# Registers loaded once per stretch, and another layout of buffers and last writes, in a two-layer graph network kernel on one Trainium2 core

## The chip, the cores and the metric

The kernel runs on one core of one Trainium2 chip. The metric is the device time of one execution in microseconds (us), taken over several executions. Engines are named as in the profile: PE (matrix products), PEld (its weight loads), DVE (VectorE), ACT (ScalarE), POOL (GpSimd), SP (SyncE, which here only issues DMAs). "ACTq", "DVEq" and "POOLq" are the instruction queues of these engines: work that a queue does itself, such as loading registers from SBUF.

## The reference

There are 6250 nodes with 128 features, and 200,000 edges with 128 features each, sorted by their destination node. `dst` is 6250 times the square of a uniform number, so low nodes have many edges. Cut to what matters:

```python
def layer0(h, edge, src, dst, W, b):
    agg_src  = segment_sum(h[src], dst, 6250)
    agg_edge = segment_sum(edge, dst, 6250)
    return relu(concat([h, agg_src, agg_edge], 1) @ W.T + b)

def sage(h, src, dst, W_l, b, W_r):
    agg = segment_sum(h[src], dst, 6250) / maximum(degree(dst), 1)
    return agg @ W_l + b + h @ W_r

h = relu(layernorm(x));  x = x + layer0(h, edge_attr, src, dst, W, b)
h = relu(layernorm(x));  h = relu(sage(h, ..., W1_l, b1, W1_r))
x = x + relu(sage(h, ..., W2_l, b2, W2_r))
```

All three layers sum over the same edges. A matrix of counts (how many edges go from node s to node d) can therefore be built once and multiplied with each layer's features.

## The kernel before

**Two stages.** The *build* (0 to about 717 us) makes the count matrix and writes it to DRAM (`counts_d`), sums the edge features per destination (`aggE`), and computes the first layer's node products. The *layers* (from about 726 us) read the count matrix back, one block of 128 destinations at a time, 49 blocks for each of three layers, and multiply it with the features.

**Groups, units, stretches.** The edges are cut into 196 groups of 1024, each of 8 tiles of 128 edges. A *unit* is n tiles that share one window of destinations: n is 4 for groups 0 to 27, 2 for groups 28 to 83 and 1 for groups 84 to 195. For each group DVE makes one-hots (`onehots`, L440; `weigh`, L450): `sp` of the source's place in its block and `sq` of destination and block. PE multiplies them (L597; L609 adds what the tile before carries over when n is 1) into the PSUM tile `pu`, which holds two units; there are three such tiles. A count of three source blocks is packed into one 32-bit word, so a destination has 17 words (NJ).

ACT copies each unit's window from `pu` into a *ring*, an SBUF tile of up to 210 destinations (L624 for n = 1; L629, with L619 and an addition on POOL at L627, for n of 2 or 4). Where it goes in the ring depends on the data, so the place is a register, loaded from `at_i` by `group_values` (L433), once for each group: 8 neighbouring registers for n = 1, every second or fourth element of `at_i` for n of 2 or 4. For n above 1 POOL loads the same places for its additions. A *stretch* is as many groups as fill one ring: 14, 7, 4, 3 or 2; in the last six regions of 14 groups, 3, 3, 3, 3 and 2. At its end POOL writes the ring to `counts_d` (L647), from the stretch's first node, which it loads with `value` (L428). The rings rotate over three buffers. Ring writes overlap in DRAM, so each waits until the one before has landed. There are 70 of them. For the very last one the ring is cleared first (L559).

**Edge sums.** Beside the counts, `edge_sums` loads 512 KB of edge features per group on SP's queue (L482, five buffers), multiplies them by a one-hot on PE (L493, tile `pe`), and DVE adds the result into `aggE` at a place from a register (L498), loaded with `value` for each group (L428). `sum_edges` sets the order of these products among the count products on PE. One block of the first layer's node products follows every third group, until group 145.

**Between the stages.** The build's pools are closed and the layers' pools opened in the same SBUF: `terms` (features as a high and a low part, split by ACT at L704 and by DVE or POOL at L706, with two columns of ones set at L662), `loads` (three blocks of counts, read by `load_counts`, L505, on SP), `wides` (blocks widened to fp32 by DVE and ACT, L697). A tile of the new pools waits for what used its bytes before. Block 0's counts go into `c_early`, a tile of its own, read on POOL's queue after stretch EARLY - 1. The last six stretches are left out of that wait; a test on the data (`bad`) makes sure that they begin behind block 0, and otherwise all is computed again by `general`, another function, which does not run on these inputs. `neighbours` then multiplies, 49 products for each block (L753), and `windows_right`, whose first loads and memsets (L835 to L856) stand early in POOL's queue, tests the windows.

The order of instructions on each engine is set by the scheduler of the framework, by dependences and program order.

Of the kernel before, what the change touches and what calls it, by code (L numbers as in the profile page):

```python
# [23 lines left out]
P = 128  # L24
D = 128
U = 8
# [10 lines left out]
NONE = 2047.0  # L37
RUN = 14
XB = 4


REGIONS = (
# [20 lines left out]
def kernel(ctx: ExitStack, tc: tile.TileContext, x, srcl, dstl, edge, w0t, b0, w1l, b1, w1r, w2l, b2, w2r, out):  # L63
# [32 lines left out]
    for g0, g1, *reg in regions:  # L96
        for g in range(g0, g1, reg[2]):
            stretches.append((g, min(reg[2], g1 - g), *reg))
    NS = len(stretches)
    EARLY = NS - 6  # L100

# [86 lines left out]
    si = 0  # L188
    for g0, g1, n, w, k, sw, win in regions:
        nc.gpsimd.memset(room[:, g0:g1], float(sw - w))  # L190
        m = -(-(g1 - g0) // k)
        nc.gpsimd.memset(most[:, si : si + m], float(sw - 1))
        si += m
    make_identity(nc, ident)
# [146 lines left out]
    for end, u in ((0, 0), (GU + 1, GU - 1)):  # L341
# [3 lines left out]
    nc.vector.memset(worse, 0.0)  # L345

    nc.vector.tensor_scalar(
        bad[:, 1:2], starts[:, NS - 1 : NS], -1.0, float(NC * P - stretches[-1][5]), op0=ALU.mult, op1=ALU.add
    )
    nc.vector.tensor_scalar(  # L350
        bad[:, 3:4], starts[:, EARLY : EARLY + 1], -1.0, float(P), op0=ALU.mult, op1=ALU.add
    )
    setup.close()

# [58 lines left out]
    ring_of = [rings.tile([P, SWMAX * NJ], I32, name=f"ring{i}") for i in (2, 1)]  # L413
# [5 lines left out]
    ring_of.append(rings.tile([P, SWMAX * NJ], I32, name="ring0"))  # L419
    padded.append(rings.tile([P, HP], F32, name="hot2"))  # L420
    ring_of.reverse()
    padded.reverse()
    for t in ring_of[:1] + padded + ring_of[1:]:
        nc.gpsimd.memset(t.bitcast(F32), 0.0)
    bpsum = build.enter_context(tc.tile_pool(name="bpsum", bufs=2, space=bass.MemoryType.PSUM))

    def value(ap, engine, most):
        return nc.values_load(  # L428
            ap, engines=[engine], min_val=0, max_val=most, skip_runtime_bounds_check_because="clamped on the chip"
        )  # L430

    def group_values(ap, engine, most):
        _, values = nc.values_load_multi_w_load_instructions(  # L433
            ap, engines=[engine], min_val=0, max_val=most, skip_runtime_bounds_check_because="clamped on the chip"
        )
        return values
# [17 lines left out]
    def carries():  # L454
# [19 lines left out]
            carry[:, 0:1], flat_q[:, T1 - 2 : T1 - 1], pu[:, 0:1].unsqueeze(2).to_broadcast([P, 1, 2]), op=ALU.subtract  # L474
        )

    def edge_sums(g):
# [12 lines left out]
        ps = bpsum.tile([P, 512], F32, name="pe", bufs=2)  # L490
        for u in range(U):
            behind = yield
            mm = nc.tensor.matmul(ps[:, :P], e[:, u, :], hot[:, u * win : u * win + P], start=u == 0, stop=u == U - 1)  # L493
# [10 lines left out]
    def load_counts(queue, c, b):  # L504
        return queue.dma_start(c, counts_d[:, b * P * NJ : (b + 1) * P * NJ].rearrange("p (d k) -> p d k", k=NJ))  # L505
# [49 lines left out]
    for si, (g0, ng, n, w, k, sw, win) in enumerate(stretches):  # L555
        nq = NJ * w
        ring = ring_of[si % 3]
        if si == NS - 1:
            nc.gpsimd.memset(ring[:, : sw * NJ].bitcast(F32), 0.0)  # L559
        if before is not None and n > 1:  # L560
# [2 lines left out]
        for g in range(g0, g0 + ng):  # L563
# [8 lines left out]
                weigh(sq[:, :, :even], g, even)  # L572
            else:
                weigh(sp, g, P)
            places = at_i[0:1, g * U : (g + 1) * U : n]
            to_put = group_values(places, ET.Activation, (sw - w) * NJ)
            if n > 1:
                to_add = group_values(places, ET.Pool, (sw - w) * NJ)
            else:

                of_first = 2 if g == G1 else 1
                sc = hots.tile([P, U + 1, NJ + NJ % 2], BF16, name="sc")
                c0 = g * U - T1 + 1
                onehots(
                    sc[:, 2 - of_first : U + 1], carry[:, c0 + 1 - of_first : c0 + U], U + of_first - 1, NJ + NJ % 2
                )
            live = [t for t in range(0, U, n) if g < G - 1 or (t + n) * P > unused]
            many = 2 if nq <= 512 else 1
            for j in range(0, len(live), many):
                units = live[j : j + many]  # L590
                pu = bpsum.tile([P, 2 * 512], F32, name="pu", bufs=3)
                for i, t0 in enumerate(units):
                    for t in range(t0, t0 + n):
                        c = i * 512
                        while c < i * 512 + nq:
                            z = min(c // 512 * 512 + 512, i * 512 + nq)
                            mm = nc.tensor.matmul(  # L597
                                pu[:, c:z],
                                sp[:, t, :],
                                sq[:, t, c - i * 512 : z - i * 512],  # L600
                                start=t == t0,
                                stop=t == t0 + n - 1 and (n > 1 or c > i * 512),
                            )
                            c = z
                    if n == 1:

                        slot = t0 + 1 if t0 != live[0] else 1
                        for j0, (sp_b, t) in enumerate(last_tiles):
                            mm = nc.tensor.matmul(  # L609
                                pu[:, i * 512 : i * 512 + NJ],  # L610
                                sp_b[:, t, :],
                                sc[:, slot + 1 - len(last_tiles) + j0, :NJ],
                                start=False,
                                stop=j0 == len(last_tiles) - 1,
                            )
                    last_tiles = [(sp, t) for t in range(t0, t0 + n)]
                if n > 1:
                    fore = hots.tile([P, 2, NJ], I32, name="fore", bufs=8)
                    nc.scalar.copy(  # L619
                        fore[:, : len(units), :], pu.rearrange("p (i c) -> p i c", c=512)[:, : len(units), :NJ]  # L620
                    )
                for i, t0 in enumerate(units):
                    if n == 1:
                        nc.scalar.copy(ring[:, bass.ds(to_put[t0], nq)], pu[:, i * 512 : i * 512 + nq])  # L624
                        continue
                    to = ring[:, bass.ds(to_add[t0 // n], NJ)]
                    add = nc.gpsimd.tensor_tensor(to, to, fore[:, i, :], op=ALU.add)  # L627
                    tc.add_to_no_dep_group(f"add{si}", add.ins)
                    put = nc.scalar.copy(  # L629
                        ring[:, bass.ds(to_put[t0 // n] + NJ, nq - NJ)], pu[:, i * 512 + NJ : i * 512 + nq]  # L630
                    )
# [12 lines left out]
            begin = 0  # L644
        else:
            begin = value(first_i[0:1, g0 : g0 + 1], ET.Pool, N - 1) * NJ
        write = nc.gpsimd.dma_start(counts_d[:, bass.ds(begin, sw * NJ)], ring[:, : sw * NJ])  # L647
# [552 lines left out]
```

## Time and profile before

| what | value |
|---|---|
| time, median of 3 runs | 1696.02 us (1693.77 to 1696.36) |
| profiled execution | 1698.32 us; its span 1696.7 us |
| granted TensorE clock, mean | 0.977 |
| PE busy | 1561.9 us (92%) |
| DVE busy | 1303.3 us (77%) |
| ACT busy | 869.3 us (51%) |
| POOL busy | 297.3 us (18%) |
| groups 0 to 27 (n = 4), by the span | 48 to 115 us |
| groups 28 to 83 (n = 2) | 115 to 303 us |
| groups 84 to 195 (n = 1) | 303 to 717 us |
| last edge product to first product of block 1 | 715.7 to 744.0 us |

The profile is of one execution. Busy time counts what an engine computes; register loads, branches, semaphores and DMA issues are not counted, though they take an engine's queue. The "chain" is the work that ended last, followed back from the last instruction, at each step to what released it. In a list of waits the three numbers are us in total, times, and the longest. In the order of time an instruction's line has its start, its length, and in brackets how long its engine idled before it and who ended that.

### The profile page before, as it was taken

Reading aid. Unit: us, or ns where it says so; the run is one execution under the profiler, and the core shown is the slowest. Engines: PE = TensorE matmul, PEld = TensorE weight load, DVE = VectorE, ACT = ScalarE, POOL = GpSimd, SP = SyncE. Lnnn points to the kernel's source line nnn. Section 1 sums busy time; section 2 is a strip of 40 time slices with the busy share of each in tenths; the row PEclk is TensorE's granted clock in tenths of the full one; section 3 lists DMA queues with packets and bytes.
Section 4 is the critical chain, followed back from the end, with each engine's and each line's share of the span. In section 5 each row is a group of like instructions: output and inputs, shape, how many; then the busy total and the mean of one; then the engine's idle time right before and its main releaser. Section 6 shows DMA issues by size and latency. Waiting matters only on the chain.

```text
span 1696.7 us, 38957 instructions
## 1 busy us (share of the span) xinstructions
PE 1561.9 (92%) x13563; PEld 1506.6 (89%) x13563; DVE 1303.3 (77%) x2810; ACT 869.3 (51%) x2183; POOL 297.3 (18%) x657
## 2 busy tenths in 40 slices
PE   5998887889988888779999999899999999999998
PEld 5897777778878877669999999899999999999998
DVE  9887776678878778777777777888676777777775
ACT  3434443566766666655555555554444453444442
POOL 2534555200000000131211222201000020000000
PEclk9999998999999999979999999999999999999999
DMA  1877766678877788766666567455555556666662
GB/s 61 261 255 252 246 224 220 237 259 278 284 274 273 276 294 311 270 230 209 199 204 214 199 222 227 169 185 199 196 189 202 185 174 206 228 219 220 221 223 97
DMA packets 122572, 377.02 MB, mean 222 GB/s; under 512 B 15249, under 2 KB 67151, under 8 KB 99712
## 3 DMA queue, kind: packets, MB, share of 16 engines
q1 hardware_dynamic: 98676, 289.00, 51.2%
q0 software_dynamic: 15088, 80.80, 12.9%
q10 hardware_dynamic: 8604, 4.66, 0.9%
q8 instruction: 109, 1.79, 0.4%
q14 instruction: 95, 0.78, 0.2%
HBM read 289.94 MB, written 84.45 MB: 221 GB/s over the span
## 4 chain that ended last, share of the span: by engine, by line
PE 69%; ACT 11%; issue 7%; ACTq 4%; DVE 4%; DMA 3%; POOL 1%; POOLq 1%; DVEq 0%
PE ps L753 50%; PE pe L493 10%; ACT ring L624 9%; ACTq L433 4%; PE pu L597 3%; DMA counts_d<-ring 3%; PE pz L394 2%; PE pu L394 1%; PE pt L296 1%; PE pt L387 1%; PE ps L751 1%; ACT ring L629 0%; DVE sq L440 0%; DVE sp L440 0%; DVE w_n L247 0%
## 5 line engine op out<-in xcount | busy, mean ns | idle before, releaser
L753 PE MATMUL ps<-terms,wide 128*128 128x256 f32 (+1 forms) x7203 | 939.7, 290 | 20.0 <-DVE terms L706 13.0
L753 PEld LDWEIGHTS ps<-terms,wide 128*128 128x128 f32 x7203 | 905.5, 198 | 26.4 <-issue 13.2
L697 DVE CAST wide<-c 128x1024 fp32r<-128x1024 uint8 (+1 forms) x584 | 524.2, 907 | 145.8 <-PE ps L753 145.3
L697 ACT CAST wide<-c 128x1024 fp32r<-128x1024 uint8 x292 | 361.5, 1238 | 294.3 <-PE ps L753 233.5
L493 PE MATMUL pe<-hot,edge_t 128*128 128x128 f32 x3136 | 490.2, 293 | 8.8 <-DVE aggE L498 5.0
L493 PEld LDWEIGHTS pe<-hot,edge_t 128*128 128x128 f32 x3136 | 406.2, 196 | 15.2 <-DVE aggE L498 6.2
L624 ACT CAST ring<-pu 128x170 f32 (+6 forms) x891 | 256.1, 289 | 135.3 <-PE pu L609 57.4
L597 PE MATMUL pu<-sq,sp 128*128 128x136 bf16 (+8 forms) x1563 | 200.3, 225 | 61.5 <-ACT ring L624 37.3
L597 PEld LDWEIGHTS <-sp 128*128 128x128 bf16 x1563 | 135.6, 100 | 32.4 <-issue 25.8
L440 DVE TENSOR_TENSOR sp<-iota,p_e 128x1024 bf16<-128x1024 f16 x196 | 134.9, 688 | 37.5 <-PE pu L597 20.6
L440 DVE TENSOR_TENSOR sq<-iota,q_e 128x1088 bf16<-128x1088 f16 (+8 forms) x196 | 141.8, 723 | 13.2 <-PE pu L609 12.1
L398 POOL DMA_DIRECT2D r_d<-r x98 | 53.4, 545 | 506.4 <-DVE r L397 484.3
L609 PEld LDWEIGHTS <-sp 128*128 128x128 bf16 x892 | 80.7, 97 | 57.9 <-issue 51.6
L627 POOL TENSOR_TENSOR ring<-ring,fore 128x17 int32 x280 | 101.8, 363 | 116.0 <-ACT fore L619 37.8
L609 PE MATMUL pu<-sc,sp 128*128 128x17 bf16 x892 | 112.5, 173 | 0.0
L629 ACT CAST ring<-pu 128x119 f32 (+5 forms) x280 | 65.8, 245 | 75.8 <-issue 34.1
L647 POOL DMA_DIRECT2D counts_d<-ring x70 | 37.9, 542 | 374.5 <-ACT ring L624 310.4
L450 DVE TENSOR_TENSOR sp<-sp,w_e 128x1024 bf16<-128x1024 bf16 x140 | 95.9, 685 | 0.0
L484 DVE TENSOR_TENSOR hot<-iota,rel 128x64 f32<-128x64 f16 (+13 forms) x196 | 94.2, 484 | 0.0
L498 DVE TENSOR_TENSOR aggE<-aggE,pe 128x8 f32 (+13 forms) x196 | 37.7, 193 | 56.7 <-PE pe L493 38.2
L397 DVE TENSOR_TENSOR r<-pz,b_sb 128x128 f32<-128x128 f32 x98 | 28.0, 286 | 67.1 <-ACT feats L395 66.7
L772 DVE TENSOR_REDUCE y<-ps 128x128 f32<-128x256 f32 x147 | 60.9, 415 | 8.4 <-PE ps L753 8.4
(167 smaller groups left out, 961.1 us busy)
## 6 DMA issues: line engine op xcount, KB each, us to landing
c<-counts_d SPq DMA_DIRECT2D x146, 1088.0 KB, 5.0
edge_t<-in_edge SPq DMA_DIRECT2D x196, 512.0 KB, 4.6
own<-r_d SPq DMA_DIRECT2D x147, 64.0 KB, 1.8
counts_d<-ring POOLq DMA_DIRECT2D x5, 1785.0 KB, 7.9
counts_d<-ring POOLq DMA_DIRECT2D x5, 1598.0 KB, 8.2
counts_d<-ring POOLq DMA_DIRECT2D x5, 1462.0 KB, 8.0
counts_d<-ring POOLq DMA_DIRECT2D x5, 1377.0 KB, 6.2
r_d<-r POOLq DMA_DIRECT2D x98, 64.0 KB, 2.1
```

The costliest lines, as they stand in the source:

```text
L433: _, values = nc.values_load_multi_w_load_instructions(ap, engines=[engine], min_val=0, max_val=most, skip_runtime_bounds_check_because="c ...
L440: nc.vector.tensor_tensor(to.rearrange("p t (c two) -> p t c two", two=2), iota[:, :m].rearrange("p (c two) -> p c two", two=2).unsqueeze( ...
L450: nc.vector.tensor_tensor(pairs, pairs, w_e[:, g].bitcast(BF16).unsqueeze(2).to_broadcast([P, U, m // 2, 2]), op=ALU.mult)
L484: nc.vector.tensor_tensor(hot[:, : U * win].rearrange("p (u w) -> p u w", w=win), iota[:, :win].unsqueeze(1).to_broadcast([P, U, win]), re ...
L493: mm = nc.tensor.matmul(ps[:, :P], e[:, u, :], hot[:, u * win : u * win + P], start=u == 0, stop=u == U - 1)
L597: mm = nc.tensor.matmul(pu[:, c:z], sp[:, t, :], sq[:, t, c - i * 512 : z - i * 512], start=t == t0, stop=t == t0 + n - 1 and (n > 1 or c ...
L609: mm = nc.tensor.matmul(pu[:, i * 512 : i * 512 + NJ], sp_b[:, t, :], sc[:, slot + 1 - len(last_tiles) + j0, :NJ], start=False, stop=j0 == ...
L624: nc.scalar.copy(ring[:, bass.ds(to_put[t0], nq)], pu[:, i * 512 : i * 512 + nq])
L627: add = nc.gpsimd.tensor_tensor(to, to, fore[:, i, :], op=ALU.add)
L629: put = nc.scalar.copy(ring[:, bass.ds(to_put[t0 // n] + NJ, nq - NJ)], pu[:, i * 512 + NJ : i * 512 + nq])
L697: copy(t[:, : p1 - p0], two)
L753: dense = nc.tensor.matmul(ps[:, :m], wide[i, q][:, p, :, two], terms[:, s, :m], start=s == 0, stop=s == NB - 1)
```

## The change

The diff has six parts.

1. The places of a whole stretch are loaded into registers by one instruction at its first group (on ACT, and on POOL for n above 1), not by one for each group. An instruction loads up to 28 registers.
2. `edge_sums` loads the first nodes of 14 groups by one instruction on DVE.
3. The last stretch (groups 194 and 195) is cut in two, of one group each, so there are 71. The very last write takes 64 destinations and not 210.
4. The pools are opened in another order: edge tiles and the one-hots' tiles first, rings last, so that `terms` and `loads` lie where no ring was.
5. The one-hots' pool (`hots`, for `sp`, `sq` and `sc`) has three buffers in place of two.
6. The count loads of blocks 1 to 3 no longer wait for the last six ring writes; the test on the data now asks that these begin behind the first four blocks of the order (nodes 0 to 639).

```diff
+TAIL = 64
+AHEAD = 4
+FIRSTS = 14
...
+    g, ng, *reg = stretches.pop()
+    stretches += [(g, ng - 1, *reg), (g + ng - 1, 1, *reg)]
     NS = len(stretches)
     EARLY = NS - 6
...
     nc.vector.tensor_scalar(
-        bad[:, 1:2], starts[:, NS - 1 : NS], -1.0, float(NC * P - stretches[-1][5]), op0=ALU.mult, op1=ALU.add
+        bad[:, 1:2], starts[:, NS - 1 : NS], -1.0, float(NC * P - TAIL), op0=ALU.mult, op1=ALU.add
     )
     nc.vector.tensor_scalar(
-        bad[:, 3:4], starts[:, EARLY : EARLY + 1], -1.0, float(P), op0=ALU.mult, op1=ALU.add
+        bad[:, 3:4], starts[:, EARLY : EARLY + 1], -1.0, float((max(order[:AHEAD]) + 1) * P), op0=ALU.mult, op1=ALU.add
     )
...
+    edges = build.enter_context(tc.tile_pool(name="edges", bufs=5))
+    zeroed = build.enter_context(tc.tile_pool(name="zeroed", bufs=1))
+    hots = build.enter_context(tc.tile_pool(name="hots", bufs=3))
     rings = build.enter_context(tc.tile_pool(name="rings", bufs=1))
-    hots = build.enter_context(tc.tile_pool(name="hots", bufs=2))
-    edges = build.enter_context(tc.tile_pool(name="edges", bufs=5))
...
-    padded = [rings.tile([P, HP], F32, name=f"hot{i}") for i in range(2)]
...
+    padded = [zeroed.tile([P, HP], F32, name=f"hot{i}") for i in range(3)]
+    ring_of = {(NS - i) % 3: rings.tile([P, SWMAX * NJ], I32, name=f"ring{i}") for i in (3, 2, 1)}
...
-        base = value(first_i[0:1, g : g + 1], ET.DVE, N - 1)
-        to = aggE[:, bass.ds(base, win)]
+        if g % FIRSTS == 0:
+            bases[:] = group_values(first_i[0:1, g : min(g + FIRSTS, G)], ET.DVE, N - 1)
+        to = aggE[:, bass.ds(bases[g % FIRSTS], win)]
...
+        wide_write = sw if si < NS - 1 else TAIL
...
-            places = at_i[0:1, g * U : (g + 1) * U : n]
-            to_put = group_values(places, ET.Activation, (sw - w) * NJ)
-            if n > 1:
-                to_add = group_values(places, ET.Pool, (sw - w) * NJ)
-            else:
+            if g == g0:
+                places = at_i[0:1, g0 * U : (g0 + ng) * U : n]
+                to_put = group_values(places, ET.Activation, (sw - w) * NJ)
+                if n > 1:
+                    to_add = group_values(places, ET.Pool, (sw - w) * NJ)
+            if n == 1:
...
-                        nc.scalar.copy(ring[:, bass.ds(to_put[t0], nq)], pu[:, i * 512 : i * 512 + nq])
+                        nc.scalar.copy(ring[:, bass.ds(to_put[(g - g0) * U + t0], nq)], pu[:, i * 512 : i * 512 + nq])
...
-        write = nc.gpsimd.dma_start(counts_d[:, bass.ds(begin, sw * NJ)], ring[:, : sw * NJ])
+        write = nc.gpsimd.dma_start(counts_d[:, bass.ds(begin, wide_write * NJ)], ring[:, : wide_write * NJ])
         if si >= EARLY:
             tc.declare_no_dep(write.ins, group="early", reason="it begins behind the first block, or all is computed again")
+            tc.add_to_no_dep_group("behind", write.ins)
...
-        load_counts(nc.sync, c, blocks[i][1])
+        load = load_counts(nc.sync, c, blocks[i][1])
+        if i < AHEAD:
+            tc.declare_no_dep(load.ins, group="behind", reason="they begin behind these blocks, or all is computed again")
```

More of the change, by code (lines that the diff above doesn't have):

```diff
@@ L190 @@
         nc.gpsimd.memset(room[:, g0:g1], float(sw - w))
-        m = -(-(g1 - g0) // k)
+        m = sum(g0 <= s[0] < g1 for s in stretches)
         nc.gpsimd.memset(most[:, si : si + m], float(sw - 1))
@@ L406, in load_x @@
         return xt
+    edges = build.enter_context(tc.tile_pool(name="edges", bufs=5))
+    zeroed = build.enter_context(tc.tile_pool(name="zeroed", bufs=1))
+    hots = build.enter_context(tc.tile_pool(name="hots", bufs=3))
     rings = build.enter_context(tc.tile_pool(name="rings", bufs=1))
-    hots = build.enter_context(tc.tile_pool(name="hots", bufs=2))
-    edges = build.enter_context(tc.tile_pool(name="edges", bufs=5))
-    ring_of = [rings.tile([P, SWMAX * NJ], I32, name=f"ring{i}") for i in (2, 1)]
     HP = U * WINMAX + P - WINMAX
     HP += HP % 2
-    padded = [rings.tile([P, HP], F32, name=f"hot{i}") for i in range(2)]
[L419 to L423, printed above, removed]
+    padded = [zeroed.tile([P, HP], F32, name=f"hot{i}") for i in range(3)]
+    ring_of = {(NS - i) % 3: rings.tile([P, SWMAX * NJ], I32, name=f"ring{i}") for i in (3, 2, 1)}
+    for t in [ring_of[0], *padded, ring_of[1], ring_of[2]]:
         nc.gpsimd.memset(t.bitcast(F32), 0.0)
@@ L475, in carries @@
         )
+    bases = []
     def edge_sums(g):
@@ L623 @@
                     if n == 1:
-                        nc.scalar.copy(ring[:, bass.ds(to_put[t0], nq)], pu[:, i * 512 : i * 512 + nq])
+                        nc.scalar.copy(ring[:, bass.ds(to_put[(g - g0) * U + t0], nq)], pu[:, i * 512 : i * 512 + nq])
                         continue
-                    to = ring[:, bass.ds(to_add[t0 // n], NJ)]
+                    to = ring[:, bass.ds(to_add[((g - g0) * U + t0) // n], NJ)]
                     add = nc.gpsimd.tensor_tensor(to, to, fore[:, i, :], op=ALU.add)
@@ L629 @@
                     put = nc.scalar.copy(
-                        ring[:, bass.ds(to_put[t0 // n] + NJ, nq - NJ)], pu[:, i * 512 + NJ : i * 512 + nq]
+                        ring[:, bass.ds(to_put[((g - g0) * U + t0) // n] + NJ, nq - NJ)], pu[:, i * 512 + NJ : i * 512 + nq]
                     )
```

## The prediction

> **What bounds the kernel now.** The page's chain first, then the same chain for the part that the change touches most, 303 to 717 us, where one tile makes one unit (n = 1). Its line shares:
>
> ```profile
> PE ps L753 50%; PE pe L493 10%; ACT ring L624 9%; ACTq L433 4%; PE pu L597 3%; DMA counts_d<-ring 3%; PE pz L394 2%; PE pu L394 1%; PE pt L296 1%; PE pt L387 1%; PE ps L751 1%; ACT ring L629 0%; DVE sq L440 0%; DVE sp L440 0%; DVE w_n L247 0%
> ```
> ```profile
> by line: ACT ring L624 37.3%; PE pe L493 18.9%; ACTq L433 11.7%; issue 11.6%; PE pu L597 6.6%; DMA counts_d<-ring 4.0%; PE pu L394 1.5%; ACT h L376 1.2%; PE pu L609 1.0%; ACTq L624 0.8%; DVE sq L440 0.8%; DMA x_c<-in_x 0.8%; DVE sp L440 0.6
> ```
>
> Half the span is the layers (L753, PE alone, from 744 us on); no instruction there changes. In the n = 1 part ACT's ring copies lead, and ACTq L433, the loading of registers in ACT's queue, holds 11.7% of 414 us = 48 us of the chain. PE's waits from 302 to 717 say who pays:
>
> ```profile
> PE pu L597 <- ACT ring L624: 37.3, 64, 2.4
> ```
>
> Why a load of eight registers is sometimes long: one stretch of three groups, ACT's and POOL's order of time, then busy times by group (length; PE, PEld, DVE, ACT, POOL; clock; DMA share; GB/s).
>
> ```profile
> L433 ACTq TENSOR_LOAD <-at_i x4: 546/548/2152, 594.8 to 605.7; - x4
> ```
> ```profile
> 595.56 2.63 ACT L624 CAST ring<-pu 128x170 f32 x8 [0.45 <-PE pe L493]
> 600.25 2.63 ACT L624 CAST ring<-pu 128x170 f32 x8 [2.06 <-issue]
> 603.32 2.63 ACT L624 CAST ring<-pu 128x170 f32 x8 [0.45 <-PE pe L493]
> ```
> ```profile
> 595.40 0.53 POOL L647 DMA_DIRECT2D counts_d<-ring  x1 [10.45 <-ACT ring L624]
> ```
> ```profile
> 594.80:597.90 3.10, 3.10 (x38) 2.85 (x34) 2.95 (x7) 2.42 (x9) 0.53 (x1) 1.00 0.63 153
> 597.90:602.60 4.70, 3.23 (x38) 2.85 (x33) 3.04 (x7) 2.42 (x9) 0.00 (x0) 1.00 0.98 397
> 602.60:605.65 3.05, 3.05 (x36) 2.80 (x33) 2.90 (x7) 2.38 (x9) 0.00 (x0) 1.00 0.81 290
> ```
>
> The load that opens a stretch takes 0.55 us: the last ring write has landed and the next is not yet moving. The second group's load, 2.5 us after POOL issued the write, takes 2.15 us: the DMA queue of the ring writes holds 65% of the engines just then. ACT pauses 2.06 us, PE idles 1.47. With a short load a group takes 3.05 to 3.10 and PE never idles. By the trace's load records the three places of a stretch average 0.55, 1.81 and 0.69 us (last six regions); all 112 loads sum to 114 us where 0.547 each would be 61.
>
> **The change, part by part.** (1) *ACT's registers, n = 1.* 112 loads become 45: 24 of 24 registers, 19 of 16, 2 of 8, each at a stretch's head, in the quiet place. Price of 24 neighbouring registers: one takes 0.30 (L428 on DVE), eight 0.547, so 35 ns for each further one: 1.11 us; 16: 0.83. Bounds: 0.55 (length is free) and three eights, 1.64. The quiet place lasts about 2.1 us (last copy 0.3, POOL's issue 0.53, 1.2 until bytes move), so I take 1.11. The stretch then needs on ACT 24 copies 0.332 apart in the chain's order of time = 7.97, a restart of 0.42 and 0.56 more load = 8.95 us; on PE 3.10 + 3.23 + 3.05 = 9.38; on DVE 8.89. It took 10.85: PE would set 9.4.
>
> All PE idle in this part is (152.4 - 133.8) + (261.8 - 226.7) = 54 us (windows 302.8 to 455.2 and 455.2 to 717): the upper end. Lower end: ACT still decides, and of the chain's 48 us the new loads keep 24 x 0.81 + 19 x 0.53 + 2 x 0.25 = 30 (length less the 0.30 behind the last copy): gain 18. PE decides in my stretch, but ACT and DVE are within 5% of it, and from 455 us DMA is busy 0.81 of 261.8 = 212 us, a floor. I take 36, two thirds of 54.
>
> A rule speaks against this. Row: 4 registers apart from each other (n = 2) take 0.89, 2 take 0.474, so 0.21 to 0.24 each, but 8 neighbours 0.547, 0.07 each. The Trainium skill, "Runtime: NRT & Kernel Launch", section "Instruction fetch mechanics", has a register load cost about 200 ns per register "even for bulk". By it a 24-register load would be 4.8 us and the 896 registers 179 us instead of the 114 traced: some 65 us slower. The row of eight is a third of the rule, so the sum goes by the row.
>
> (2) *DVE's first_i, 14 at a time.* 182 of 196 loads go. Short ones (0.30) hide behind the one-hots ahead; the long ones (1.29 at 608.7) fall in the same writes as ACT's. Nothing added to (1): they are inside PE's idle sum. A 14-register load is 0.76 (0.30 to 2.4 by strided rows), 14 times: nothing. *The third one-hot buffer* removes waits of DVE for PE: of `sp` and `sq` (L440) 26 us from 300 to 717. PE itself waited for DVE only 6.7 us there (aggE 5.0, r 1.4, hot 0.3), which bounds the gain; a loss would need more work, and there is none. It mostly keeps DVE's 8.89 off a 9.4 path: 2 won (0 to 7).
>
> (3) *n = 4 and n = 2 (48 to 303 us).* As many registers as before, apart from each other, so no cheaper: 28 cost about 6 us, 16 about 3.5, 8 about 1.8, in lumps. The first lump, 6 us from 45 on POOL and 47 on ACT, lies beside 6.15 us of edge products on PE (48.6 to 54.8), which wait for neither: nothing, and 3 us lost if that cover is short. In n = 2 ACT's lump of 3.5 us holds up PE only beyond the three pu tiles, 1.5 groups, 4.3 us. POOL's lump stands behind its write's issue, where loads of four already take 1.6 to 2.5 us; queued behind it are the ring additions and the next write. Loads hold 6.8% + 3.3% of 187 us = 19 us of this part's chain. Bounds: half of that won, 10; or 23 stretches each half a us later, 12 lost. Taken: 2 won.
>
> (4) *The handover.* Before, everything waited for the last ring write:
>
> ```profile
> 711.26 8.09 DMA counts_d<-ring
> 719.98 5.96 DMA counts_d<-ring
> 732.19 4.69 DMA limits_d<-limit
> 740.07 3.92 PE ps L753 x18
> ```
>
> PE ends the build at 715.7; the write lands at 725.9; block 0 stalls on POOL's two splits (behind rows, limit) at half clock; block 1 begins at 743.9. In the built order of the change, splits and ones column no longer wait for rings, but every *widened* piece of block 0, on DVE and ACT, still waits for the last write, and there is one write more. The write of 194 is still 210 wide and cannot go before 719.4, when its predecessor lands; ahead of it on POOL stand the ones column and four row loads (2.7 us from 715.9), which fit. Three loads of 1088 KB run beside it from 717: 3.34 + 1.83 MB at the 0.42 MB/us of the windows 728 to 734 end at 729.3, or at 726 if the write goes first. Then the short write: 557 KB = 1.33 us plus the 1.6 that 5.96 leaves over 1.83 MB: about 3. It lands between 729 and 734; I take 732. The first piece is there 0.85 later, block 0 takes 8.0 (20 products at the half clock's 0.218, 3.92 over 18; 29 at 0.122, as later blocks have them), block 1 begins near 741: 2.5 won, between 2 lost and 6 won. The early loads themselves win little: block 1's were there in time before too.
>
> Sum: 36 + 2 + 2 + 2.5 = 42.5. Profiled execution 1698.3 less 42.5 = 1655.8; it lies 2.3 over the median shown: 1653.5, given as 1654.
>
> **Rivals.** (a) *DMA and DVE take over.* A group's DMA work, 2.8 to 3.2 us from 455 us on, meets a period of 3.1; writes then lag, edge tiles come late. Against it: PE idles least in groups with short loads, though DMA is 0.63 to 0.81 busy there. Gain 8 to 28, near 1678. 0.20. (b) *Slower: a register costs the same alone or in bulk.* If each beyond the eighth costs the strided 0.22, a 24-register load is 4.1 us, 1 us more than a stretch's three loads now (3.05), and in one lump longer than PE's lead of three pu tiles (six of eight units, 2.3 us); 43 stretches x about 1 us, and n = 2 no better: near 1735. It decides from 0.16 us per further register. For it the strided rows; against it the row of eight. 0.08. (c) *More than PE's share returns*: with no long pauses the half-clock spells go too (clock 0.90 from 197 to 303), gain 58 to 66, near 1634. 0.07. (d) *It does little*: loads stay as long in sum, contention moves with them, POOL's lumps take the rest: within 4 of 1696, either side. 0.05. Forecast (gain 28 to 58): 0.60.
>
> **How the numbers follow.** 0.2%, 3.4 us, is about what a measurement can tell from no change. Faster: 0.60 + 0.20 + 0.07 = 0.87; same 0.03, slower 0.02 from (d); slower 0.08 from (b). The range takes in most of (a) and the forecast's bounds, leaving out (b), part of (c) and the ends of (a) and (d): 1635 to 1685.
>
> **What would show it.** Right: ACT's L433 loads in n = 1 near 1 us, none of 2 us between copies of one stretch; PE's wait for L624 from 37 us to under 12; build's end near 679; block 1 beginning 25 to 27 us after it (28.2 before). Wrong: 24-register loads over 2 us; the three-group stretch still over 10 us with PE waiting for edge tiles or ACT for ring writes; the last write landing over 18 us after PE's last edge product.

## The result, and the profile after

The changed kernel is slower: 1719.7 us (median of 4 runs, 1716.6 to 1723.0) against 1695.9, a ratio of 1.0143 (95% interval 1.0120 to 1.0167). The forecast was 1654, in a range of 1635 to 1685. The profiled execution took 1721.56 us with a span of 1720.0, 23.3 longer than before's 1696.7. Cut where VectorE starts the edge one-hots (`hot`) of groups 0, 28, 84 and 195:

| part | before, us | after, us | difference |
|---|---|---|---|
| ahead of group 0 | 48.3 | 50.9 | +2.6 |
| n = 4 | 67.1 | 81.2 | +14.1 |
| n = 2 | 187.3 | 212.5 | +25.2 |
| n = 1, to group 195 | 407.7 | 387.3 | -20.4 |
| handover and layers | 986.3 | 988.1 | +1.8 |

So n = 1 gained, though 20 us where about 38 had been forecast, and more than that was lost in the two parts that had been put at 2 us won. The 2.6 us ahead of group 0 are GpSimd's first load, of 28 registers. By the load records it ends at 50.87 us, and VectorE starts group 0's `hot` at 50.92; the first edge products wait for it. PE's wait from 48 to 75 us:

```profile
PE pe L495 <- DVE hot L486: 2.9, 1, 2.9
```

Of the kernels tried below, the two that keep this load, e2 and e5, start that `hot` at 50.4 and 51.2 us, all others at 47.4 to 48.8.

The page's chain by line, the chain of the n = 1 part (345 to 737 us), and PE's waits in it:

```profile
PE ps L761 50%; PE pe L495 12%; ACT ring L629 5%; ACTq L433 3%; PE pu L602 3%; PE pz L399 2%; DMA counts_d<-ring 1%; DVE sp L440 1%; PE pt L301 1%; DVE sq L440 1%; PE pu L399 1%; PE pt L392 1%; PE ps L759 1%; DVE hot L486 1%; POOLq L428 0%
```
```profile
by line: PE pe L495 35.9%; ACT ring L629 20.6%; PE pu L602 10.7%; issue 10.1%; ACTq L433 7.0%; DMA counts_d<-ring 3.2%; PE pu L399 2.4%; DVE hot L486 1.9%; PE pu L614 1.5%; DVE sp L440 1.3%; DVEq L433 1.3%; DVE sq L440 1.0%; ACT hT L394 0.9
```
```profile
PE pu L602 <- ACT ring L629: 19.0, 33, 3.9
PE pe L495 <- DVE hot L486: 7.1, 10, 4.2
```

Over the span ACT's copies fell from 9% to 5%, and from 345 to 737 us they lost the lead to PE (20.6% against 37.3% before), its register loads fell from 11.7% to 7.0%, and PE's wait for the copies halved. New is a wait for VectorE's one-hots, up to 4.2 us at once. The loads from 590 to 640 us (minimum, median, maximum in ns), ACT's order of time in three stretches of three groups there (windows as wide as in the prediction's stretch), and busy times of the first two (columns as there):

```profile
L433 ACTq TENSOR_LOAD <-at_i x6: 1022/1488/1584, 589.3 to 637.6; - x6
```
```profile
604.87 8.00 ACT L629 CAST ring<-pu 128x170 f32 x24 [1.39 <-PE pu L614]
614.26 7.95 ACT L629 CAST ring<-pu 128x170 f32 x24 [1.39 <-PE pu L614]
623.61 8.04 ACT L629 CAST ring<-pu 128x170 f32 x24 [1.40 <-PE pu L614]
```
```profile
604.50:613.87 9.37, 9.22 (x104) 8.85 (x103) 8.81 (x20) 7.22 (x24) 0.53 (x1) 1.00 0.92 330
613.87:623.22 9.35, 8.73 (x98) 8.40 (x98) 8.61 (x20) 7.22 (x24) 0.53 (x1) 1.00 0.91 328
```

Each stretch is one run of 24 copies behind one load of 1.5 us, 9.35 to 9.39 us from start to start, where it was 10.85. The forecast period of 9.4 us is there, but in part by luck: ACT's queue alone fills it, with 8.00 us of copies and a pause of 1.39 under the load, 9.39, where the sum had 8.95. PE, which was to set it, is busy for 9.22 and 8.73 us of it.

VectorE's loads of 14 registers in n = 1 (minimum, median, maximum in ns), what it does at one of them, and PE beside it, in order of time:

```profile
L433 DVEq TENSOR_LOAD <-first_i x8: 1316/2616/6736, 357.8 to 685.4; - x8
```
```profile
686.82 0.23 DVE L440 TENSOR_TENSOR sc<-iota,carry 128x144 bf16<-128x144 f16 x1
692.13 0.23 DVE L501 TENSOR_TENSOR aggE<-aggE,pe 128x74 f32 x1 [5.09 <-issue]
```
```profile
693.11 1.22 PE L495 MATMUL pe<-hot,edge_t 128*128 128x128 f32 x4 [4.22 <-DVE hot L486]
```

"issue" is time in which the profile shows no awaited event; by the trace's load records it is the load of `first_i` (6.51 us from 685.4). The next group's `hot`, `sp` and `sq` are queued behind it, so PE runs dry for 4.22 us.

The lengths follow the place in `first_i`. By the load records the seven loads that begin at groups 0, 28, 56 and so on took 1.32 to 2.06 us, and the seven between them, at groups 14, 42, 70 and so on, 3.18 to 6.74. Two of these (3.40 us at 90.3 and 3.18 at 298.1) overlap no packet of a ring write. In e1 below the same two sets took 1.31 to 2.31 and 3.18 to 4.26. What it is about the place is not shown.

In n = 2 (132 to 345 us), the chain, then PE's wait for ring copies:

```profile
by line: issue 46.2%; PE pe L495 11.4%; ACTq L433 10.3%; PE pu L602 4.4%; POOL ring L632 3.6%; POOLq L428 3.5%; POOLq L632 3.3%; POOLq L433 3.1%; ACT ring L634 3.0%; DVE sp L440 2.0%; DVE sq L440 1.6%; DVEq L433 1.2%; ACT fore L624 0.9%; DV
```
```profile
PE pu L602 <- ACT ring L634: 30.3, 18, 3.5
```

Nearly half of that chain is time for which the profile has no cause (26.1% before); the wait was 18.2 us before.

Not all of the loss in n = 4 and n = 2 is waiting. Both parts before, then after (columns as in the prediction):

```profile
48.00:115.00 67.00, 66.52 (x661) 63.76 (x659) 58.69 (x189) 27.45 (x123) 31.29 (x65) 0.96 0.82 264
115.00:303.00 188.00, 157.22 (x1403) 144.85 (x1402) 141.26 (x398) 77.58 (x411) 95.85 (x252) 0.95 0.71 239
```
```profile
51.00:132.00 81.00, 72.53 (x688) 68.21 (x689) 57.44 (x206) 27.12 (x138) 27.88 (x63) 0.94 0.64 216
132.00:345.00 213.00, 165.31 (x1371) 151.43 (x1371) 138.54 (x376) 76.06 (x400) 90.03 (x252) 0.92 0.61 206
```

On as many products (2064 before, 2059 after) PE is busy for 237.8 us against 223.7, at a lower granted clock (0.94 and 0.92 against 0.96 and 0.95). So of the 39 us lost 14 are longer busy time of PE and 25 are idle time. No run takes the clock apart from the pauses: whether these lower it stays open.

The handover, from the chain, and PE's first product of the layers:

```profile
734.71 6.98 DMA counts_d<-ring
742.35 12.15 DMA counts_d<-ring
757.95 1.58 DMA limits_d<-limit
```
```profile
759.51 0.55 PE L761 MATMUL ps<-terms,wide 128*128 128x258 f32 x1 [22.37 <-DMA limits_d<-limit]
```

The write of group 194 takes 12.15 us beside the three early count loads, where the write of the same width took 5.96. The short write is issued at 755.14 and is there about 3 us later, some 21 us after PE's last edge product (737.1). The last line names `limits_d`, which lands just as the first widened piece is done (VectorE starts it at 758.61). PE stands idle for 22.37 us; the second block starts 30.5 us after the last edge product (28.2 before).

### The profile page after: what moved, and what is told of

Read it like the earlier page. It is cut to its first block, busy times and chain, and to the rows that moved or that the text cites. A ratio compares the mean times of both kernels' runs of the same rounds, so it can differ in the third digit from the quotient of the medians.

```text
span 1720.0 us, 38616 instructions
## 1 busy us (share of the span) xinstructions
PE 1569.6 (91%) x13563; PEld 1518.6 (88%) x13563; DVE 1296.1 (75%) x2810; ACT 868.0 (50%) x2183; POOL 291.3 (17%) x658
## 4 chain that ended last, share of the span: by engine, by line
PE 71%; issue 9%; ACT 6%; DVE 6%; ACTq 4%; DMA 2%; POOLq 1%; POOL 1%; DVEq 0%
PE ps L761 50%; PE pe L495 12%; ACT ring L629 5%; ACTq L433 3%; PE pu L602 3%; PE pz L399 2%; DMA counts_d<-ring 1%; DVE sp L440 1%; PE pt L301 1%; DVE sq L440 1%; PE pu L399 1%; PE pt L392 1%; PE ps L759 1%; DVE hot L486 1%; POOLq L428 0%
## 5 line engine op out<-in xcount | busy, mean ns | idle before, releaser
L761 PE MATMUL ps<-terms,wide 128*128 128x256 f32 (+1 forms) x7203 | 936.7, 290 | 25.2 <-DMA limits_d<-limit 22.4
L495 PE MATMUL pe<-hot,edge_t 128*128 128x128 f32 x3136 | 505.7, 299 | 16.2 <-DVE hot L486 10.0
L495 PEld LDWEIGHTS pe<-hot,edge_t 128*128 128x128 f32 x3136 | 420.3, 201 | 24.1 <-DVE hot L486 12.0
L629 ACT CAST ring<-pu 128x170 f32 (+6 forms) x891 | 257.0, 288 | 116.3 <-PE pu L614 68.3
L632 POOL TENSOR_TENSOR ring<-ring,fore 128x17 int32 x280 | 95.5, 341 | 165.2 <-ACT ring L634 79.9
L634 ACT CAST ring<-pu 128x68 f32 (+5 forms) x280 | 65.3, 244 | 68.1 <-issue 63.8
L624 ACT CAST fore<-pu 128x34 int32<-128x34 f32 x140 | 26.8, 191 | 90.6 <-PE pu L602 56.8
```

Of the source, the lines that this page charges most:

```text
L629: nc.scalar.copy(ring[:, bass.ds(to_put[(g - g0) * U + t0], nq)], pu[:, i * 512 : i * 512 + nq])
L634: put = nc.scalar.copy(ring[:, bass.ds(to_put[((g - g0) * U + t0) // n] + NJ, nq - NJ)], pu[:, i * 512 + NJ : i * 512 + nq])
L761: dense = nc.tensor.matmul(ps[:, :m], wide[i, q][:, p, :, two], terms[:, s, :m], start=s == 0, stop=s == NB - 1)
```

## The experiments

Each was timed beside the kernel before, which took 1699.75, 1698.45 and 1696.79 us (medians) in the three sessions. Where sessions are compared, the ratio to before is used, 1% of it being 17 us. The parts are those of the table above, from one profiled execution each; e1's and e3's lie 10 and 5 us below the medians of those kernels. Kernels whose ACT and POOL load group by group in n = 4 and n = 2 took 65.9 to 68.9 us in n = 4 (e1, with 73.8, apart) and 179.9 to 193.2 in n = 2.

| kernel | median, us | ratio to before, 95% | n = 4 | n = 2 | n = 1 | rest |
|---|---|---|---|---|---|---|
| before | 1695.9 | 1 | 67.1 | 187.3 | 407.7 | 986.3 |
| after | 1719.7 | 1.0143 (1.0120 to 1.0167) | 81.2 | 212.5 | 387.3 | 988.1 |
| e1_n1_only | 1678.4 | 0.9874 (0.9858 to 0.9891) | 73.8 | 179.9 | 378.7 | 987.4 |
| e2_dve_each | 1695.4 | 0.9979 (0.9957 to 1.0000) | 69.1 | 211.5 | 375.5 | 988.3 |
| e3_both | 1667.5 | 0.9810 (0.9793 to 0.9826) | 68.8 | 185.9 | 371.7 | 986.5 |
| e4_no_regs | 1696.6 | 0.9985 (0.9970 to 0.9999) | 68.6 | 184.0 | 406.5 | 987.4 |
| e5_pool_lump | 1684.4 | 0.9924 (0.9901 to 0.9946) | 68.6 | 199.6 | 374.0 | 987.0 |
| e6_act_lump | 1693.2 | 0.9974 (0.9956 to 0.9991) | 73.1 | 208.7 | 372.9 | 989.2 |
| e7_neighbours | 1665.3 | 0.9812 (0.9783 to 0.9841) | 67.4 | 190.6 | 366.4 | 989.2 |
| e8_firsts4 | 1666.7 | 0.9808 (0.9773 to 0.9842) | 67.4 | 193.2 | 371.0 | 989.1 |
| e9_late_loads | 1658.3 | 0.9781 (0.9757 to 0.9804) | 68.3 | 187.6 | 370.9 | 982.4 |
| e10_short_clear | 1657.1 | 0.9782 (0.9759 to 0.9805) | 68.9 | 190.2 | 363.4 | 981.7 |
| e11_before_n1 | 1670.4 | 0.9852 (0.9830 to 0.9875) | 66.4 | 186.8 | 381.8 | 984.4 |
| e12_two_hots | 1675.4 | 0.9873 (0.9850 to 0.9897) | 65.9 | 188.2 | 380.7 | 989.0 |

**Which part costs: four kernels that undo the loads part by part.** In e1 the loads of n = 4 and n = 2 go back to one for each group:

```diff
-            if g == g0:
-                places = at_i[0:1, g0 * U : (g0 + ng) * U : n]
-                to_put = group_values(places, ET.Activation, (sw - w) * NJ)
-                if n > 1:
-                    to_add = group_values(places, ET.Pool, (sw - w) * NJ)
+            if n > 1:
+                places = at_i[0:1, g * U : (g + 1) * U : n]
+                to_put = group_values(places, ET.Activation, (sw - w) * NJ)
+                to_add = group_values(places, ET.Pool, (sw - w) * NJ)
+            elif g == g0:
+                to_put = group_values(at_i[0:1, g0 * U : (g0 + ng) * U], ET.Activation, (sw - w) * NJ)
...
```

The rest of the edit counts the places of n = 4 and n = 2 from the group and not from the stretch.

> The changed kernel, but where n is 4 or 2 (groups 0 to 83) ScalarE's and GpSimd's registers are loaded group by group as before; n = 1 stays per stretch, and VectorE still loads 14 firsts at a time. The changed kernel took 1719.7 us, 23.8 more than before: 39 us more in n = 4 and n = 2 (81.2 + 212.5 against 67.2 + 187.3), 20.4 less in n = 1, 2.6 more ahead of the build and 2.3 more in the handover. Theory LUMPS (the loads of registers that stand apart, 28, 14, 16 and 12 in one piece, hold up ScalarE and GpSimd): the 39 us come back nearly whole, n = 4 near 68, n = 2 near 189, the whole near 1682. Rival FIRSTS (VectorE's load of 14 neighbours, 1.3 to 6.7 us, is what stops the build in every part): most of the 39 stays, near 1710. Rival ORDER (the new layout, the third one-hot buffer and the order that they give make every part slower, whatever the loads): near 1715.

Measured 1678.4: LUMPS' total, but not its parts: n = 2 came back (179.9), n = 4 only half way (73.8).

In e2 VectorE loads one register for each group again:

```diff
-        if g % FIRSTS == 0:
-            bases[:] = group_values(first_i[0:1, g : min(g + FIRSTS, G)], ET.DVE, N - 1)
-        to = aggE[:, bass.ds(bases[g % FIRSTS], win)]
+        base = value(first_i[0:1, g : g + 1], ET.DVE, N - 1)
+        to = aggE[:, bass.ds(base, win)]
```

> The changed kernel, but VectorE loads one first_i for each group as before; ScalarE's and GpSimd's loads stay per stretch in all parts. LUMPS: only the long loads of VectorE beside ring writes come back, 14 loads with 3 to 4 us of idle TensorE beside half of them, some 10 to 20 us less their cover: 1705 to 1715. FIRSTS: 1690 to 1700, with n = 4 and n = 2 near the times before. ORDER: within 4 us of 1719.7.

Measured 1695.4, the total that FIRSTS gave, but again with other parts: n = 2 stayed at 211.5, while n = 4 fell by 12.1 us and n = 1 by 11.8. So neither theory alone: the lumps own n = 2, VectorE's load owns n = 1's loss, and most of n = 4's loss needs both (81.2 with both, 69.1 with lumps alone, 73.8 with VectorE's load alone).

e3 is both edits together:

> Both of the two edits above: only n = 1's ScalarE registers are loaded per stretch; layout, third one-hot buffer, short last write and early count loads stay. LUMPS with FIRSTS as a second cause: n = 4 near 68, n = 2 near 188, n = 1 between 370 and 380, the whole 1665 to 1675. LUMPS alone: as without the VectorE edit, near 1682. ORDER: above 1705.

Measured 1667.5, as the two causes together give it. e4 also loads n = 1's places for each group again:

```diff
-            elif g == g0:
-                to_put = group_values(at_i[0:1, g0 * U : (g0 + ng) * U], ET.Activation, (sw - w) * NJ)
...
-                        nc.scalar.copy(ring[:, bass.ds(to_put[(g - g0) * U + t0], nq)], pu[:, i * 512 : i * 512 + nq])
+                        nc.scalar.copy(ring[:, bass.ds(to_put[t0], nq)], pu[:, i * 512 : i * 512 + nq])
```

> The changed kernel without its register part: all loads group by group as before; what is left of the change is the layout (first layer buffers free of rings), the third one-hot buffer, the short last ring write and the early count loads. LUMPS and FIRSTS: near the kernel before, 1692 to 1700, with the handover 2 us longer than before and n = 1 near 405. ORDER: above 1710. If the third one-hot buffer frees VectorE as the prediction had it, n = 1 falls by 2 us.

Measured 1696.6, so ORDER is out: without its loads the change is worth -0.15% (-0.3 to 0). In ratios the sum is: layout and the rest -2.5 us; n = 1's loads on ACT per stretch (e4 to e3) -30; lumps in n = 4 and 2 (e3 to e2) +29; VectorE's fourteen (e3 to e1) +11; and 17 more where both of these meet (after against e3 is 57, not 40). Each is good to about 3 to 6 us, by the intervals.

**Which engine's lump.** On e3, one engine loads per stretch where n is 4 or 2, the other per group. e5:

```diff
-                to_add = group_values(places, ET.Pool, (sw - w) * NJ)
+                if g == g0:
+                    to_add = group_values(at_i[0:1, g0 * U : (g0 + ng) * U : n], ET.Pool, (sw - w) * NJ)
...
```

> On the kernel with only n = 1's ScalarE registers per stretch (1667.5 us; its n = 2 part 185.8 us): in n = 4 and n = 2 GpSimd's registers alone are loaded per stretch, ScalarE's group by group. With both engines per stretch n = 2 took 211.5 and the whole 1695.4, so the lumps cost 28. Theory ACT (ScalarE's lump stops the copies that free TensorE's pu tiles): at most 6 us of the 28 are here, 1667 to 1674. Rival POOL (GpSimd's lump, queued behind the ring write and ahead of the ring additions, makes additions and the next write late): most of it is here, 1685 to 1695, n = 2 near 205.

Measured 1684.4, by ratios 19 us above e3: far above ACT's band and just short of POOL's. e6 does the same to ACT's places, and leaves POOL's per group:

```diff
-                to_put = group_values(places, ET.Activation, (sw - w) * NJ)
+                if g == g0:
+                    to_put = group_values(at_i[0:1, g0 * U : (g0 + ng) * U : n], ET.Activation, (sw - w) * NJ)
...
```

> The mirror of it: in n = 4 and n = 2 ScalarE's registers alone are loaded per stretch, GpSimd's group by group. ACT: 1685 to 1695, n = 2 near 207, TensorE waiting for ScalarE's first copies of a stretch. POOL: 1667 to 1674. If both come to about half (1678 to 1684 each) the two costs add; if both stay under 1674 the cost arises only where both lumps read at the same time as a ring write.

Measured 1693.2, by ratios 28 above e3, as theory ACT had it. So ACT's lumps alone cost as much as both (29 in e2), and POOL's alone cost 19: the two costs overlap. The waits in n = 2 show two routes. For ACT, PE's waits (us in total, times, longest) in e3, then in e2 and e6:

```profile
PE pu L602 <- ACT ring L634: 13.1, 14, 2.6
```
```profile
PE pu L601 <- ACT ring L633: 37.0, 16, 5.4
```
```profile
PE pu L603 <- ACT ring L635: 29.3, 18, 3.6
```

and VectorE's, in e3, e2 and e6:

```profile
DVE r L402 <- ACT feats L400: 6.0, 4, 2.1
```
```profile
DVE r L402 <- ACT feats L400: 34.0, 10, 5.1
```
```profile
DVE r L402 <- ACT feats L400: 21.5, 9, 4.1
```

PE waits 24 us more for ring copies in e2 and 16 more in e6, and the first layer's `feats`, which ACT computes in the same queue, come late too. Yet ACT's loads take less time in sum. ACT's and POOL's loads in n = 2 (minimum, median, maximum in ns), in e3 and in e2:

```profile
L433 ACTq TENSOR_LOAD <-at_i x56: 885/892/3167, 119.4 to 302.6; - x56
L433 POOLq TENSOR_LOAD <-at_i x53: 935/982/2641, 116.0 to 301.3; - x53
```
```profile
L433 ACTq TENSOR_LOAD <-at_i x23: 1712/1735/4916, 118.4 to 326.1; - x23
L433 POOLq TENSOR_LOAD <-at_i x22: 2441/3105/5437, 120.5 to 330.1; - x22
```

By the load records for groups 28 to 83, ACT's sum to 61.9 us in e3, 52.9 in e2 and 55.7 in e6; POOL's to 71.8, 78.9 and 72.9. In e6 both together are 5 us less than in e3, and the part is 23 us longer: what counts is the length of one piece. For POOL the place is worse as well: in after all 17 of its loads from 100 to 300 us overlap a ring write's packets, since they stand right behind its issue; before, 30 of 58 did. In e5 ACT's queue and the copies stay short, and the loss shows in POOL's additions, which wait 47.6 us for "issue" (21.4 in e3).

**Is it registers that stand apart?** e7, on e3:

```diff
-                places = at_i[0:1, g * U : (g + 1) * U : n]
+                every = n if n > 2 else 1
+                places = at_i[0:1, g * U : (g + 1) * U : every]
...
-                    to = ring[:, bass.ds(to_add[t0 // n], NJ)]
+                    to = ring[:, bass.ds(to_add[t0 // every], NJ)]
```

(and the same for `to_put`).

> On the same kernel (1667.5 us): in n = 2 each group's load takes 8 neighbouring registers in place of every second one, 4 that stand apart, and uses every second; n = 4 as it was. In the kernel before, 8 neighbours took 0.547 us and 4 apart 0.89 to 0.95, on 112 loads. If standing apart is what costs: loads of n = 2 near 0.55 us, ScalarE's and GpSimd's sums of 68 and 74 us fall by a third, n = 2 from 186 to 175 to 181, the whole 1657 to 1663. If the number of registers is what costs, the loads double to 1.8 us and the whole is 1680 or more. If the loads are hidden, within 3 of 1667.5.

```profile
L433 ACTq TENSOR_LOAD <-at_i x56: 537/550/2041, 116.7 to 303.2; - x56
L433 POOLq TENSOR_LOAD <-at_i x54: 561/568/1499, 118.9 to 304.3; - x54
```

Twice the registers in 0.6 of the time, as the first theory had it, and the sums for groups 28 to 83 fell from 61.9 to 40.6 us and from 71.8 to 36.7. The time did not move (0.9812 against 0.9810), so its forecast of 1657 to 1663 missed and the third reading holds. A load of 0.9 us for each group was already covered in n = 2; only a longer one shows.

**VectorE's length or its neighbours?** e8 is e3 with the changed kernel's loads of `first_i`, four at a time:

```diff
-FIRSTS = 14
+FIRSTS = 4
...
-        base = value(first_i[0:1, g : g + 1], ET.DVE, N - 1)
+        if g % FIRSTS == 0:
+            bases[:] = group_values(first_i[0:1, g : min(g + FIRSTS, G)], ET.DVE, N - 1)
...
```

> On the same kernel (1667.5 us; with VectorE's firsts 14 at a time 1678.4): VectorE's firsts 4 at a time, 49 loads in place of 196 or 14. Theory LENGTH (a lump of 14, 1.3 to 4.3 us, is longer than the lead of the one-hots over TensorE; a short one is not): loads of 0.42 us quiet, 1 to 1.5 beside a write, the whole 1664 to 1669. Rival CONTENTION (any load of several neighbours beside a ring write stops VectorE for 3 us or more): 1672 to 1682, as with 14.

Measured 1666.7: LENGTH. VectorE's longest load in n = 1 is 1.68 us, and PE's wait for one-hots is 3.2 us, none over 0.3. Loads of four all begin at a multiple of four groups, which only every second load of 14 did; so the run shows that short loads do no harm, but not why every second long one took over 3 us, and no run loads 12 or 16 at a time. But 147 loads fewer on VectorE win nothing against one for each group either.

**The handover.** e9, on e3, is one constant, which makes the count loads wait again:

```diff
-AHEAD = 4
+AHEAD = 1
```

> On the kernel with only n = 1's ScalarE registers per stretch (1667.5 us): the layers' first count loads on SP's queue wait for the last ring write again, so none runs beside the write of 194. There that write took 12.9 us from issue to landing, against 5.96 in the kernel before, and its landing releases the short write. Theory SHARED (the early loads take its bandwidth): 5.5 to 7 us again, the short write issued when GpSimd's splits end, some 6 us earlier, the whole 1660 to 1663. Rival NEEDED (block 1 then waits for its own count loads): block 0 earlier, but a stall of 4 to 6 us ahead of block 1, the whole 1665 to 1669.

The write's issue-to-landing (last number, us), POOL's order of time, and PE's first product:

```profile
counts_d<-ring POOLq DMA_DIRECT2D x2, 1785.0 KB, 5.9
```
```profile
684.37 5.55 POOL L714 TENSOR_TENSOR terms<-feats,terms 128x1024 fp32r<-128x1024 f32 x2 [0.27 <-ACT terms L712]
689.87 0.53 POOL L847 DMA_DIRECT2D rows<-unit_d  x1
690.39 0.58 POOL L652 DMA_DIRECT2D counts_d<-ring  x1
```
```profile
694.73 0.55 PE L761 MATMUL ps<-terms,wide 128*128 128x258 f32 x1 [14.74 <-DMA limits_d<-limit]
```

SHARED holds: 5.9 us again, and the short write now waits for POOL's splits, not for the write. PE's idle is 14.74 us, where e3's was 20.95, and the second block starts 23.8 us after the last edge product against 29.1. The time fell by 9 by medians and 5 by ratios, whose intervals overlap a little; the 5.3 us of the two profiles agree with that.

e10 adds to e9 a clear of the last ring over its 64 written places alone:

```diff
-            nc.gpsimd.memset(ring[:, : sw * NJ].bitcast(F32), 0.0)
+            nc.gpsimd.memset(ring[:, : TAIL * NJ].bitcast(F32), 0.0)
```

> The same, and the last ring is cleared only over the 64 places that are written, not over 210: the memset of 3.08 us, between the landing of one write and the issue of the next on GpSimd, becomes about 0.9. If that row is on the path: 2 us less than with the late loads alone, 1658 to 1661. If the short write then waits for GpSimd's splits (5.6 us, queued ahead of it) and not for the write of 194: within 1 us of it. Hypothesis to beat: this is the fastest version.

1657.1 and 0.9782: the same as e9. The memset fell from 3.08 to 1.00 us, but the short write still stands behind the splits. These two are the fastest versions: about 2.2% below the kernel before, some 60 us below the changed one.

**The gain by itself, and the third buffer.** e11 is the kernel before with n = 1's places loaded per stretch, and nothing else:

```diff
             places = at_i[0:1, g * U : (g + 1) * U : n]
-            to_put = group_values(places, ET.Activation, (sw - w) * NJ)
+            if n > 1:
+                to_put = group_values(places, ET.Activation, (sw - w) * NJ)
+            elif g == g0:
+                to_put = group_values(at_i[0:1, g0 * U : (g0 + ng) * U], ET.Activation, (sw - w) * NJ)
...
```

> The kernel before with one edit: n = 1's ScalarE registers per stretch. If the layout, the third one-hot buffer, the short write and the early loads are worth nothing to the build, it saves what it saved there, 29 us (1696.5 to 1667.5): 1667 to 1671 beside 1698. If the gain needs the third one-hot buffer (VectorE, at 8.89 us a stretch, would be the next bound): 1675 to 1685.

Measured 1670.4, by ratios 25 us less than before: inside the band of the first reading, some 5 short of the gain in e3. e12 is e3 with two buffers for `hots`:

```diff
-    hots = build.enter_context(tc.tile_pool(name="hots", bufs=3))
+    hots = build.enter_context(tc.tile_pool(name="hots", bufs=2))
```

> The kernel with only n = 1's ScalarE registers per stretch (1667.5 us), but two one-hot buffers in place of three. The prediction gave the third 2 us (0 to 7): 1667 to 1674 without it. If TensorE never waits for VectorE there: within 2 of 1667.5.

Measured 1675.4, by ratios 11 us above e3, more than either theory gave. In the n = 1 part of e12:

```profile
PE pu L602 <- ACT ring L629: 19.1, 35, 2.4
PE pu L602 <- DVE sp L450: 4.5, 7, 0.9
```

PE waits 4.5 us for weighted one-hots, a wait that is not among e3's, and the part takes 9.0 us longer, of which the waits explain half; in e11, also with two buffers, it takes 381.8. So the third buffer pays, but only once n = 1's places are loaded per stretch: with the loads as before, n = 1 is 406.5 with it (e4) and 407.7 without (before).

## Why the prediction was wrong, point by point

**(1) n = 1 on ACT: right in size, the reason in part by luck.** Forecast 36 (18 to 54). Measured 35 in the n = 1 part of the profiles (406.5 in e4, 371.7 in e3) and 30 by ratios. The load of 24 neighbouring registers took 1.49 us where nothing disturbed it, not 1.11, within its bounds (0.55 to 1.64). PE's wait for copies did not fall under 12 but to 19, and in e3 too (19.2 us). Two lines of the "what would show it" list thus failed on size while the gain held. Nor does PE alone set the stretch, as the sum had it: with its longer load ACT's queue fills the same 9.4 us.

**(2) VectorE's 14 registers: the step "14 times: nothing" failed.** Its price, "0.76 (0.30 to 2.4)", was read off loads of other shapes. Seven of the 14 loads took 1.32 to 2.06 us and seven 3.18 to 6.74, two of these with no ring write beside them. The step also counted only what went away (182 short loads, covered) and gave the lump no cover of its own; behind it in VectorE's queue stand the one-hots that PE needs next. It cost 11 us alone (e1 against e3) and 28 beside the lumps (after against e2). *The third one-hot buffer* was mis-sized: 2 (0 to 7) forecast, about 11 measured. The wait that bounded it (6.7 us) was read in a kernel in which PE waited far longer for ACT (37.3), which is a likely reason.

**(3) n = 4 and n = 2: the step that failed most.** The lengths were right (8 registers apart 1.74 us against "about 1.8", 28 about 6.1). The cover was not: "ACT's lump of 3.5 us holds up PE only beyond the three pu tiles, 1.5 groups, 4.3 us". In e2 PE's wait rose by 24 us over 23 stretches, 1.0 each, at loads of 2.3 us on the mean (52.9 over 23), which puts the cover at about 1.3, an estimate. The step took PE's lead at its most, with all three tiles empty. It gave 2 won, with 12 lost as the worst; 29 were lost. That ACT's queue also holds the first layer's `hT` and `feats` was not counted at all. The first lump was to lie beside edge products that "wait for neither". They do wait: their `hot` came just behind POOL's load of 6.46 us, 2.4 us later than in e3 (50.4 in e2, 48.0 in e3), near the 3 that the text had as its bound. Behind that, n = 4 kept its length in e2 (69.1 against 68.8), though not in e6 (73.1), and lost 12 us more when VectorE's lump was added.

**(4) The handover: order right, one term mis-sized.** Short write 3.1 us (about 3) and block 0 8.1 (8.0) came as forecast. The write of 194 was to land at 726 to 729.3, at most 13.6 us after PE's last edge product. It was issued 5.2 us after that product, where the sum had 3.7: the write ahead of it had stood behind a ring clear of 3.07 us that the sum left out. It took 12.15 and landed 17.4 after. The sum gave the three loads and the write the full rate in turn; e9 shows that without the loads the write takes 5.9. So 2 lost where 2.5 were to be won. Named as a sign of error, "the last write landing over 18 us after PE's last edge product" is what happened (21).

**The rivals.** The time went to rival (b)'s side, not by its mechanism: it needed 0.16 us for each further register and 4.1 for 24; (1.488 - 0.546) / 16 = 0.059 from 8 to 24 was measured. Rival (a) is not seen: with DMA busy 0.85 of the n = 1 part, e3 kept the gain. Lumps of n = 4 and n = 2 that lose their cover were in the text as a bound of (3); of the rivals only (d), at 0.05 and near 1696, named any of them, POOL's.

**The rule weighed.** The Trainium skill, "Runtime: NRT & Kernel Launch", section "Instruction fetch mechanics", gives about 200 ns for each register "even for bulk"; that page speaks of loads from HBM, and the places here lie in SBUF. The runs come to the same figure for registers that stand apart (28 in 6.07 us on ACT, 0.22 each) and for every second of VectorE's loads of 14 neighbours (3.18 where no ring write ran, 0.23 each), and not for the other neighbours (24 in 1.49, 0.06 each).

## What to carry to other kernels

When many small waits in a queue are gathered into one, price the longest piece against the cover at the very place where it will stand, not the sum: in e6 the sum of the loads fell by 5 us and n = 2 took 23 us longer. Read that cover as what the next engine still has in hand there (its idle time after such a pause), not as the depth of the buffers between them. And list everything in the queue behind the piece: here these were VectorE's next one-hots, ACT's ring copies and first-layer steps, and POOL's ring additions.

## What was not expected of the hardware

- **A register load beside a ring write is often long.** In before the eight-register loads of n = 1 have a median of 1.73 us where they share 0.25 us or more with a write's packets (57 loads) and 0.55 elsewhere (55). VectorE's load of 6.74 us ended at 597.3, and the packets of the write beside it at 597.6; in e3 one on ACT lasted from 658.0 to 663.5, and a write's packets from 658.3 to 663.8. That both happen together is shown; what they share is not.
- **Registers side by side can be cheap:** 8 in 0.55 us and 24 in 1.49 on ACT, against 4 apart in 0.89. VectorE's 14 took 1.32 or 3.18 us with no write beside them, by where they begin.
- **POOL pays more than ACT** for the same registers in quiet, 0.94 against 0.89 for four apart.
- Why n = 4 loses 12 us where VectorE's lump and the others meet, and 0 to 5 for each alone, stays open: no run took the two apart in time.
